# Packed probability blocks, paired value products and single banks in a fused attention and feed-forward kernel

## The chip, the cores and the metric

The kernel runs on one core of a Trainium2 chip. The metric is the device time of one execution in microseconds (us), the median of the runs shown. All data are fp32 in memory; some products take their operands as fp32r, a form that TensorE reads in one pass, where fp32 takes two (two records for each product in the trace).

## The reference

x is (2, 1024, 512), that is 2048 rows of 512. One layer: causal attention with 16 heads of 32, a residual and a layer norm, then a feed-forward part with the signs of its weights, a residual and a layer norm.

```python
qkv = jnp.einsum('bsd,ed->bse', x, w_qkv) + b_qkv          # heads of 32
scores = jnp.einsum('bhqd,bhkd->bhqk', q, k) / math.sqrt(Hd) + causal
out = jnp.einsum('bhqk,bhkd->bhqd', jax.nn.softmax(scores), v)
x = layernorm(x + jnp.einsum('bsd,ed->bse', out, w_out) + b_out)
hidden = relu(jnp.einsum('bsd,hd->bsh', x, sign(up_w)) * up_scale)      # 2048 wide
x = layernorm(x + jnp.einsum('bsh,dh->bsd', hidden, sign(down_w)) * down_scale * output_scale)
```

## The kernel before

**Order.** The kernel first makes a list of tasks. Each has the engines it may run on with estimated costs, a due time (`place`), and the tiles that it reads and writes. `Plan.schedule` (from L104) plays these through, engine by engine, earliest due first, and fixes each engine's order and each tile's buffer. The instructions are then issued in that order (`tc.manual_schedule`); at run time each engine takes its own in order, with semaphore waits. A tile class has so many equal buffers (`slots`), and its tiles get them in the order of their first use. So a change of an estimate moves instructions on all engines.

**Attention** goes in 8 chunks (two batches, four groups of four heads; 128 columns of q, k and v each). For a chunk, `project` makes four L494 products for k and q (each four matmuls of 512 columns, fp32) and 32 value blocks (L531). Keys and queries are split into a high and a low fp32r part (ScalarE L571 and VectorE L576 for keys; VectorE L515, then POOL L554 and L559 for queries). `stack` copies the parts by DMA (L450) into `stacks`, where a head's four parts lie on 128 partitions: 32 DMAs a chunk. The projection of chunk c+1 runs among the attention of chunk c. Chunk 0 is cut in two: rows 0 to 511 have plain fp32 scores (L708) from unsplit k and q, so that attention can begin before stacks exist; 48 stack DMAs of 64 KB for the rest are issued alternately by SP and ScalarE (`BOTH`).

A chunk goes through 8 tiles i of 128 query rows. A tile's heads come in units of 4, 2 or 1, as i grows. For a unit: scores (L727 or L708) into one of two PSUM tiles of two banks (`d0`, `d1`); the mask (L743) and the row maximum (L753) on VectorE; Exp with its row sum on ScalarE (L759); a reciprocal (L770); the scaling of probabilities on POOL (L776); transposes on TensorE (L798) into a bank; a copy to `probsT` by ScalarE or VectorE (L432, L434). After the units of a tile, `values` issues its products as one task: 4(i+1) matmuls of 32 columns (L822), two records each, into one bank, and VectorE adds the bias (L837). `probs` has 4 buffers of 1024 columns and `probsT` 8 buffers of 8 blocks, whatever a unit needs.

**Between.** After a batch's last chunk, `output` multiplies by w_out (L875), adds the residual rows and takes statistics; `normalise` scales (L913).

**Feed-forward** goes in 4 blocks of 512 rows. For each of 16 hidden tiles: eight up-products (L987), ReLU on ScalarE (L998), a split on VectorE (L1004, L1009), and down-products (L1024) into four 512-wide halves of `d0` and `d1`, one for each 128 rows. The last hidden tiles' down-products (4 of them in the last block) come row tile by row tile. Then for each row tile: scale (L1038, VectorE), residual (L1046, on POOL; the very last on VectorE), statistics (L1052, L1057), root (L1062, ScalarE), L1068, scaling (L1073), and a DMA out. These y rows have 3 buffers. Most DMAs are issued by SP.

Of the kernel before, what the change touches and what calls it, by code (L numbers as in the profile page):

```python
# [10 lines left out]
F32 = mybir.dt.float32  # L11
# [15 lines left out]

LAG = 6.0
# [12 lines left out]
GBPS = 220.0  # L41


class Tile:


    def __init__(self, plan, cls, after=()):
        self.cls, self.after = cls, after
        self.users, self.left, self.end = [], 0, 0.0
        self.slot = None  # L50
        self.parts = {}
        self.at = len(plan.classes[cls]["tiles"])
        plan.classes[cls]["tiles"].append(self)
# [12 lines left out]
class Plan:  # L66
# [8 lines left out]
    def tile(self, cls, after=()):  # L75
        return Tile(self, cls, after)
# [33 lines left out]
    def schedule(self):  # L110
# [15 lines left out]
        dma, order = 0.0, []  # L126
        blocked = []
# [5 lines left out]
        def lacks(t, now):  # L133

            at = 0.0
            for x in t.tiles:
                if x.slot is not None:
                    continue
                c = self.classes[x.cls]
                if c["next"] != x.at or not c["free"] or c["held"] >= c["most"] or any(a.left for a in x.after):  # L140
                    return None
                at = max([at, min(c["free"])[0]] + [a.end for a in x.after])
            return at
# [5 lines left out]
        while count < len(self.tasks):  # L149
# [37 lines left out]
            for x in t.tiles:  # L187
                if x.slot is None:
                    c = self.classes[x.cls]
                    pick = min(c["free"])  # L190
                    c["free"].remove(pick)
                    x.slot = pick[1]
                    c["next"] += 1
                    c["held"] += 1
                    opened = True
# [3 lines left out]
            if t.size:  # L199
                dma = max(dma, now + 1.7) + t.size * 1.024 / GBPS  # L200
                t.end = dma
            else:
                t.end = now + until
# [13 lines left out]
            for x in t.tiles:  # L217
                x.left -= 1
                x.end = max(x.end, t.end + 0.15)
                if not x.left:  # L220
                    self.classes[x.cls]["free"].append((x.end, x.slot))
                    self.classes[x.cls]["held"] -= 1
                    opened = True
# [10 lines left out]
def kernel(  # L234
# [86 lines left out]
    def place_for(stack, name, n, kind=F32, side="left"):  # L321
# [9 lines left out]
    doubles = [psum.tile([P, 2 * TB], F32, tag=f"d{k}", name=f"d{k}") for k in range(2)]  # L331
# [14 lines left out]
        "pr": views(a_pr, (2 * TB,)),  # L346
        "pt": views(a_pt, (8, P)),
# [19 lines left out]
        "pd": [d[:, k * TB : (k + 1) * TB] for d in doubles for k in range(2)],  # L367
        "pu": singles,
        "y": views(a_v, (D,))[:3],
        "dsc": views(a_v, (D,))[3:4],  # L370
# [8 lines left out]
    def reopen(cls):  # L379

        if cls == "raw" or cls == "xt" and homes["xt"][0] is None:
            right.close()
            xt = place_for(right, "xt0", 2 * NC * TB, F32R, "right")
            homes["xt"][:1] = views(xt, (2, NC, TB), F32R)
            raw = place_for(right, "raw", NC * TB, side="right")
            homes["raw"] = views(raw, (NC, TB))
        else:
            left.close()
            xt = place_for(left, "xt1", 2 * NC * TB, F32R)
            homes["xt"][1:] = views(xt, (2, NC, TB), F32R)  # L390
            homes["hf"] = views(place_for(left, "hf", 4 * TB), (TB,))
            hid = place_for(left, "hid", 12 * TB, F32R)
            homes["hh"] = views(hid, (TB,), F32R)[:6]
            homes["hr"] = views(hid, (TB,), F32R)[6:]

    def of(t):
        if homes[t.cls][t.slot] is None:
            reopen(t.cls)
        return homes[t.cls][t.slot]

    rows_at = {"x1": views(a_x1, (NQ, D))[0], "xT": views(a_x, (NQ, D))[0]}

# [25 lines left out]
    BOTH = {"SP": (0.6, 0.6), "ACT": (0.5, 0.5)}  # L428
# [12 lines left out]
    all_of = {cls: [] for cls in homes}  # L441

    def new(cls, after=()):
        t = plan.tile(cls, [y for c in after for y in all_of[c]])
        all_of[cls].append(t)
        return t
# [196 lines left out]
    def first_half():  # L643
# [9 lines left out]
        for c in range(NC):  # L653
            dma(
                -100, lambda c=c: of(w)[:, c, 1, :], lambda c=c: w_qkvT[ts(c, P), D : D + P], 64,
                writes=[w[1, c]], queue=act_queue,
            )
# [10 lines left out]
        v, kq = new("v"), new("pt")  # L668
        rows = lambda n: of(kq)[:, 4 * n : 4 * n + 4, :].rearrange("p a b -> p (a b)")
# [6 lines left out]
    def second_half():  # L676

        kq, v = plain[0, 0]
        st, hl = new("st"), new("hl")
        place = pace(-10, 6, 16 * 3)  # L680
        split(hl, 0, lambda: of(kq)[:, 4:8, :].rearrange("p a b -> p (a b)"), [kq[1]], -20)
        stack(st, 1, hl, 0, 0, TB, lambda: -20, BOTH)
        ps = product(0, 0, 1, TB, place)
        split_keys(0, 0, hl, TB, ps, -10)
        stack(st, 1, hl, TB, TB, TB, lambda: -20, BOTH)
        ps = product(0, 0, 0, TB, place)
        qh, full = new("hl"), new("full")
        with_bias(0, 0, 0, lambda: of(full), [full[0]], ps, -10)
        split(qh, 0, lambda: of(full), [full[0]], -10)
        stack(st, 0, qh, TB, 0, TB, lambda: -20, BOTH)  # L690
        values_of(0, 0, v, TB, place)
        made[0, 0] = st, v
# [7 lines left out]
    def scores(b, e, i, heads, at):  # L700
        G, N, W = len(heads), (i + 1) * P, 2 * TB // len(heads)
        sc, nm, pr, sums = new("sc"), new("nm"), new("pr"), new("sums")
        if (b, e) in plain and i < NQ // 2:
            kq = plain[b, e][0]

            def fn(_):
                for j, u in enumerate(heads):
                    nc.tensor.matmul(  # L708
                        of(sc)[:, j * W : j * W + N],
                        lhsT=of(kq)[ts(u, HD), i, :],  # L710
                        rhs=of(kq)[ts(u, HD), 4 : 5 + i, :].rearrange("p a b -> p (a b)"),
                        start=True,
                        stop=True,
                    )
# [41 lines left out]
        for j in range(G):  # L756
# [3 lines left out]
                    of(pr)[:, j * W : j * W + N],  # L760
# [12 lines left out]
        for j in range(G):  # L773
# [3 lines left out]
                    of(pr)[:, j * W : j * W + N],  # L777
                    of(pr)[:, j * W : j * W + N],
# [9 lines left out]
    def transposes(i, heads, pr, at):  # L788
        W = 2 * TB // len(heads)
        blocks = [(j, j * W + k * P) for j in range(len(heads)) for k in range(i + 1)]  # L790
        pt = new("pt")
        for g in range(0, len(blocks), 4):
            some = blocks[g : g + 4]
            tp = new("tp")
            for k, (j, c) in enumerate(some):
# [3 lines left out]
                        of(tp)[:, k, :], of(pr)[:, c : c + P], ident  # L799
# [6 lines left out]
                lambda g_, g=g, m=m, tp=tp: copied(g_, of(pt)[:, g : g + m, :], of(tp)[:, :m, :]),  # L806
# [6 lines left out]
    def values(b, e, i, each, at):  # L813
        if (b, i) not in atT:
            atT[b, i] = new("atT")
        to, v, rows = new("po"), (made.get((b, e)) or plain[b, e])[1], atT[b, i]
        each = each[::-1]

        def fn(_):
            for k in range(i, -1, -1):  # L820
                for u, pt, c in each:
                    nc.tensor.matmul(  # L822
                        of(to)[ts(u, HD), 0, :],
                        lhsT=of(v)[:, k, ts(u, HD)],
                        rhs=of(pt)[:, c + k, :],
                        start=(k == i),
                        stop=(k == 0),
                    )

        plan.task(  # L830
            {"PE": (0.14 + 0.218 * (i + 1), 0.2 + 0.218 * (i + 1))}, fn, at,
            [v[t] for t in range(0, (i + 1) * P, TB)] + [pt[0] for _, pt, _ in each],
            updates=[to[0]], count=8 * (i + 1), label="po",
        )
        plan.task(
            dve(0.345),
            lambda _: nc.vector.tensor_scalar(  # L837
                of(rows)[:, e, :],
                of(to)[:, 0, :],
                bqk[:, 2 * NC + e : 2 * NC + e + 1],  # L840
                None,
                ALU.add,
            ),
            at - FAST, [to[0]], [rows[e]], label="at",
        )

    def attend(b, e, i, base):


# [7 lines left out]
        values(b, e, i, each, base - 2)  # L857
# [110 lines left out]
    def feed_forward(up, dn, dsc, base):  # L968
        UNIT = 2.0

        def block(tb):
# [7 lines left out]
            for f in range(NFC):  # L979
                pu, hf = new("pu"), new("hf", ["pr", "pt"])  # L980
                hh, hr = new("hh", ["pr", "pt"]), new("hr", ["pr", "pt"])
                at = start + f * UNIT
# [50 lines left out]
            for t in range(TPB):  # L1033
                y, st, m, pd, rows = new("y", ["v"]), new("st6"), new("st6"), pds[t], x1[b]
# [8 lines left out]
                adder = dve(0.692) if final and t + 1 == TPB else pool(1.264)  # L1043
                plan.task(
                    adder,
# [26 lines left out]
                    dve(0.546),  # L1072
                    lambda _, m=m, y=y: nc.vector.tensor_scalar(  # L1073
# [15 lines left out]
    for at, (b, e) in enumerate(chunks):  # L1089
# [3 lines left out]
        for i in range(NQ):  # L1093
            attend(b, e, i, base + i * (i + 1) / 2)
        if e == NC - 1:

            x1[b] = new("x1" if b < B - 1 else "xT")
            for i in range(NQ):
                there = base + (i + 1) * (i + 2) / 2 + LAG
                output(b, i, pace(there, there + 4, 16))  # L1100
# [96 lines left out]
```

## Time and profile before

| | us |
|---|---|
| median of 3 runs | 784.16 (783.38 to 786.16) |
| profiled execution, its own time | 780.83 |
| its span | 779.0 |
| attention, up to the first feed-forward product | about 523 |
| feed-forward, to the end | about 256 |

| engine | busy us |
|---|---|
| TensorE (PE) | 758.6 |
| VectorE (DVE) | 519.8 |
| ScalarE (ACT) | 378.9 |
| GpSimd (POOL) | 261.6 |

In the profile a group reads: line, engine, operation, output<-input by the program's names, shape, count. "A <- B: 2.2, 1, 2.2" among the waits means that A's engine sat idle for A until B was done: total us, times, longest. PEld is the loading of weights, which overlaps products. In the chain a piece starts where the piece before it ended, or at what released it; SPq and ACTq are DMA issues.

### The profile page before, as it was taken

The numbers are of one execution on the slowest core, as the hardware profiler recorded it, in microseconds if no ns is written. First come the engines' busy times: TensorE is split into PE (matmuls) and PEld (weight loads), VectorE is DVE, ScalarE is ACT, GpSimd is POOL, SyncE is SP. The second block draws the span as 40 slices with busy tenths as digits, with TensorE's granted clock in tenths as the row PEclk, the third lists the DMA queues.
The fourth block names the chain that finished last, engine by engine and source line by source line (L and its number), as shares of the span: only waits on it lengthen the run. The fifth ranks groups of instructions, "written<-read, shape, count | busy, mean of one in ns | idle before, by whom it ended". The sixth has DMA issues, their size and how long they took to land.

```text
span 779.0 us, 15429 instructions
## 1 busy us (share of the span) xinstructions
PE 758.6 (97%) x5864; PEld 568.4 (73%) x5864; DVE 519.8 (67%) x1083; ACT 378.9 (49%) x841; POOL 261.6 (34%) x329
## 2 busy tenths in 40 slices
PE   8899899999999999999999999999999999999994
PEld 4567768868855775786876876668777887777883
DVE  1678598688777767888878879966336337337325
ACT  1366468667644454566666678654222222222111
POOL 2336346346435443535544545440002002002001
PEclk9999999999999999999999999999999999999998
DMA  8535625226533522634504423332001001001001
GB/s 232 116 82 126 178 61 129 70 60 138 170 77 73 137 58 49 146 89 109 110 2 109 110 64 131 135 120 97 1 0 55 1 0 55 1 0 41 14 0 54
DMA packets 38120, 62.35 MB, mean 80 GB/s; under 512 B 6048, under 2 KB 18336, under 8 KB 38048
## 3 DMA queue, kind: packets, MB, share of 16 engines
q1 hardware_dynamic: 35616, 59.08, 29.5%
q10 hardware_dynamic: 2400, 2.30, 1.2%
q8 instruction: 46, 0.75, 0.4%
q14 instruction: 26, 0.21, 0.1%
q0 software_dynamic: 32, 0.01, 0.0%
HBM read 24.66 MB, written 4.19 MB: 37 GB/s over the span
## 4 chain that ended last, share of the span: by engine, by line
PE 87%; DMA 3%; SPq 3%; DVE 3%; POOL 1%; ACTq 1%; ACT 1%; issue 1%; POOLq 0%; DVEq 0%
PE s L987 15%; PE d L1024 15%; PE s L798 15%; PE s L494 12%; PE d L727 9%; PE s L822 8%; PE s L875 7%; PE s L531 6%; SPq L450 3%; DMA stacks<-wqkv 1%; ACTq L450 1%; PE s L938 1%; DVE small L753 1%; DMA xT<-in_xT 1%; DVE probsT L434 1%
## 5 line engine op out<-in xcount | busy, mean ns | idle before, releaser
L776 POOL TENSOR_SCALAR probs<-probs,small 128x128 f32<-128x128 f32 (+7 forms) x256 | 189.7, 750 | 251.9 <-DVE small L770 216.4
L759 ACT ACTIVATE probs<-d,small 128x128 f32<-128x128 f32 (+7 forms) x256 | 189.2, 749 | 90.0 <-DVE small L770 22.5
L753 DVE TENSOR_REDUCE small<-d 128x1 f32<-128x640 f32 (+9 forms) x178 | 180.0, 1016 | 2.8
L798 PE MATMUL s<-ident,probs 128*128 128x128 f32 x1152 | 164.0, 274 | 0.3 <-POOL probs L776 0.3
L798 PEld LDWEIGHTS s<-ident,probs 128*128 128x128 f32 x1152 | 133.1, 140 | 36.0 <-issue 22.9
L432 ACT COPY probsT<-s 128x512 f32<-128x512 f32 (+3 forms) x195 | 96.0, 520 | 91.1 <-PE s L798 81.6
L1024 PE MATMUL d<-stacks,hid 128*128 128x512 f32 x512 | 134.6, 399 | 0.8 <-DVE v L1038 0.8
L987 PE MATMUL s<-xt,stacks 128*128 128x512 f32 x512 | 134.2, 400 | 0.0
L727 PE MATMUL d<-stacks 128*128 128x512 f32 (+3 forms) x368 | 129.7, 437 | 4.5 <-DMA stacks<-wqkv 2.2
L494 PE MATMUL s<-xT,wqkv 128*128 128x512 f32 x256 | 129.0, 597 | 1.0 <-DMA xT<-in_xT 1.0
L998 ACT ACTIVATE hf<-s,ups 128x512 f32<-128x512 f32 x64 | 44.0, 688 | 167.1 <-PE s L987 167.1
L1024 PEld LDWEIGHTS d<-stacks,hid 128*128 128x128 f32 x512 | 93.8, 188 | 25.5 <-DVE v L1038 2.0
L1004 DVE CAST hid<-hf 128x512 fp32r<-128x512 f32 x64 | 27.4, 428 | 126.6 <-ACT hf L998 126.6
L987 PEld LDWEIGHTS s<-xt,stacks 128*128 128x128 f32 x512 | 94.4, 188 | 23.2 <-issue 1.0
L434 DVE COPY probsT<-s 128x512 f32<-128x512 f32 (+3 forms) x150 | 86.6, 592 | 19.2 <-PE s L798 16.6
L727 PEld LDWEIGHTS d<-stacks 128*128 128x128 f32 x368 | 60.0, 190 | 44.5 <-issue 26.6
L743 DVE TENSOR_TENSOR d<-d,mask 128x128 f32<-128x128 f32 (+2 forms) x178 | 62.3, 354 | 32.3 <-PE d L727 27.1
L822 PEld LDWEIGHTS s<-probsT,v 128*32 128x32 f32 x2304 | 59.0, 109 | 28.5 <-issue 7.9
L822 PE MATMUL s<-probsT,v 128*32 128x128 f32 x2304 | 76.2, 275 | 0.0
L531 PE MATMUL s<-wqkv,xT 128*128 128x128 f32 x512 | 71.3, 275 | 0.0
L531 PEld LDWEIGHTS s<-wqkv,xT 128*128 128x128 f32 x512 | 66.0, 192 | 6.5 <-issue 5.0
L875 PE MATMUL s<-wout,atT 128*128 128x512 f32 x128 | 64.5, 597 | 0.2 <-DVE xt L950 0.2
(63 smaller groups left out, 489.3 us busy)
## 6 DMA issues: line engine op xcount, KB each, us to landing
stacks<-wqkv SPq DMA_DIRECT2D x224, 128.0 KB, 2.4
wqkv<-in_w_qkvT SPq DMA_DIRECT2D x22, 256.0 KB, 3.6
xT<-in_xT SPq DMA_DIRECT2D x16, 256.0 KB, 4.5
rows<-in_x SPq DMA_DIRECT2D x16, 256.0 KB, 2.8
raw<-in_up_wT SPq DMA_DIRECT2D x4, 1024.0 KB, 5.0
out<-v SPq DMA_DIRECT2D x16, 256.0 KB, 2.0
raw<-in_down_wT SPq DMA_DIRECT2D x2, 1024.0 KB, 5.2
atT<-in_down_wT SPq DMA_DIRECT2D x2, 1024.0 KB, 6.5
```

Of the source, the lines that this page charges most:

```text
L432: nc.scalar.copy(dst, src)
L494: nc.tensor.matmul(of(ps).rearrange("p a b -> p (a b)"), lhsT=of(w)[:, c, n, :], rhs=of(xt)[:, c, t0 : t0 + TB], start=(c == 0), stop=(c = ...
L531: nc.tensor.matmul(of(ps)[:, t, :], lhsT=of(xt)[:, c, t0 + t * P : t0 + (t + 1) * P], rhs=of(w)[:, c, 2, :], start=(c == 0), stop=(c == NC ...
L727: nc.tensor.matmul(of(sc)[:, j * W + k0 : j * W + k1], lhsT=of(st)[:, 0, u, ts(i, P)], rhs=of(st)[:, 1, u, k0:k1], start=True, stop=True,)
L753: lambda _: nc.vector.tensor_reduce(of(nm)[:, :G], sc3()[:, :, :N], AX.X, ALU.max, negate=True),
L759: lambda _, j=j: nc.scalar.activation(of(pr)[:, j * W : j * W + N], of(sc)[:, j * W : j * W + N], AF.Exp, bias=of(nm)[:, j : j + 1], accum ...
L776: lambda _, j=j: nc.gpsimd.tensor_scalar(of(pr)[:, j * W : j * W + N], of(pr)[:, j * W : j * W + N], of(sums)[:, j : j + 1], 1.0, ALU.mult ...
L798: lambda _, k=k, c=c, tp=tp: nc.tensor.transpose(of(tp)[:, k, :], of(pr)[:, c : c + P], ident),
L822: nc.tensor.matmul(of(to)[ts(u, HD), 0, :], lhsT=of(v)[:, k, ts(u, HD)], rhs=of(pt)[:, c + k, :], start=(k == i), stop=(k == 0),)
L875: lambda _, c=c: nc.tensor.matmul(bank(py), lhsT=of(a)[:, c, :], rhs=of(wout)[:, c, :], start=(c == 0), stop=(c == NC - 1),),
L987: lambda _, f=f, c=c, n=n, pu=pu: nc.tensor.matmul(of(pu), lhsT=of(up)[:, f // TPB, c, ts(f % TPB, P)], rhs=of(xt)[:, n, c, :], start=(c = ...
L1024: lambda _, f=f, t=t, n=n, h=h: nc.tensor.matmul(of(pds[t]), lhsT=of(h)[:, ts(t, P)], rhs=of(dn)[:, f // 4, f % 4, :], start=(f == 0 and n ...
```

## The change

The diff has six parts.

1. **Rings.** `pr` and `pt` are no longer 4 and 8 equal buffers but rings of 32 and 64 blocks of 128 columns in the same memory. A unit takes only its G(i+1) blocks, contiguous, and blocks come free in order of taking. Exponentials are packed next to each other.
2. **Two tiles in one run.** `attend` holds back the value products of tiles 0, 2 and 4 and issues them with those of the next tile, in one task and one bank; not for tiles 0 to 3 of chunk 0. The last chunk takes its tiles in the order 0, 1, 2, 7, 6, 5, 4, 3.
3. **First stacks.** All of chunk 0's stack DMAs are issued by SP. The first key weights come in two DMAs in place of four.
4. **Single banks.** When the down-products begin, the pool of `d0` and `d1` is closed and four one-bank tiles are opened in its place.
5. **y rows** lie in the old `atT` area, 8 buffers. In the last block the residual of the first three row tiles may go to VectorE or POOL, and their scaling too. The last block's up-products are due 6 us earlier (`HURRY`).
6. **The planner** counts 200 GB/s, 2.3 us to landing and eight DMAs in flight, where it had 220, 1.7 and no limit.

The core of the diff:

```diff
+TOGETHER = (0, 2, 4)
+LAST = [0, 1, 2, 7, 6, 5, 4, 3]
+HURRY = 6.0
...
-GBPS = 220.0
+GBPS = 200.0
+LANDING = 2.3
+LANES = 8
...
+    def room(self, c, x):
+
+        live, n = c["live"], x.blocks
+        if not live:
+            return 0
+        head, tail = live[-1].slot + live[-1].blocks, live[0].slot
+        if head > tail:
+            return head if head + n <= c["ring"] else 0 if n <= tail else None
+        return head if head + n <= tail else None
...
-        "pd": [d[:, k * TB : (k + 1) * TB] for d in doubles for k in range(2)],
+        "pd": [None] * 4,
         "pu": singles,
-        "y": views(a_v, (D,))[:3],
-        "dsc": views(a_v, (D,))[3:4],
+        "y": views(a_at, (D,)),
+        "dsc": views(a_v, (D,))[:1],
...
+        elif cls == "pd":
+            wide.close()
+            narrow = wide.enter_context(tc.tile_pool(name="narrow", bufs=1, space=PSUM))
+            homes["pd"] = [
+                narrow.tile([P, TB], F32, tag=f"pd{k}", name=f"pd{k}") for k in range(4)
+            ]
...
+    rings = {
+        "pr": (a_pr, 4 * 2 * TB // P), "pt": (a_pt, 8 * 2 * TB // P)
+    }
...
-        stack(st, 1, hl, 0, 0, TB, lambda: -20, BOTH)
+        stack(st, 1, hl, 0, 0, TB, lambda: -20)
...
+        pr = new("pr", blocks=G * (i + 1))
...
-                    of(pr)[:, j * W : j * W + N],
+                    of(pr)[:, j * N : (j + 1) * N],
...
-    def values(b, e, i, each, at):
+    def values(b, e, some, at):
...
+            for n, (i, each) in enumerate(some):
+                for k in range(i, -1, -1):
+                    for u, pt, c in each[::-1]:
+                        nc.tensor.matmul(
+                            of(to)[ts(u, HD), n, :],
+                            lhsT=of(v)[:, k, ts(u, HD)],
+                            rhs=of(pt)[:, ts(c + k, P)],
+                            start=(k == i),
+                            stop=(k == 0),
+                        )
...
-        values(b, e, i, each, base - 2)
+        waiting.append((i, each))
+        if not hold_back:
+            values(b, e, waiting[:], base - 2)
+            waiting.clear()
...
-                at = start + f * UNIT
+                at = start + f * UNIT - (HURRY if final else 0)
...
-                adder = dve(0.692) if final and t + 1 == TPB else pool(1.264)
+                both = {**dve(0.692), **pool(1.264)}
+                if not final:
+                    both = pool(1.264)
                 plan.task(
-                    adder,
+                    both if t + 1 < TPB else dve(0.692),
...
+        tiles = list(range(NQ))
+        if at + 1 == len(chunks):
+            tiles = LAST
+        begin, past = {}, base
+        for i in tiles:
+            begin[i] = past
+            attend(b, e, i, past, i in TOGETHER and not (at == 0 and i < NQ // 2))
+            past += i + 1
```

## The prediction

> **What bounds the kernel now.** I read the page first: busy time by engine, then the chain that ended last.
>
> ```profile
> PE 758.6 (97%) x5864; PEld 568.4 (73%) x5864; DVE 519.8 (67%) x1083; ACT 378.9 (49%) x841; POOL 261.6 (34%) x329
> PE 87%; DMA 3%; SPq 3%; DVE 3%; POOL 1%; ACTq 1%; ACT 1%; issue 1%; POOLq 0%; DVEq 0%
> ```
>
> TensorE is busy for 97% of the span and makes 87% of the chain. The next engine is VectorE with 67%. A gain can come from three places alone: cheaper instructions in TensorE's stream, TensorE waits that go, and the ends, where TensorE has nothing to do. The table by stretch says how much lies at the ends (columns: stretch, its length, busy time with counts, granted clock, DMA share, GB/s).
>
> ```profile
> 1.00:42.00 41.00, 37.51 (x202) 22.65 (x203) 16.15 (x38) 11.14 (x36) 10.60 (x21) 1.00 0.70 183
> 523.00:763.00 240.00, 240.00 (x1056) 191.34 (x1055) 108.69 (x210) 59.02 (x92) 18.13 (x13) 1.00 0.07 23
> 763.00:779.00 16.00, 5.11 (x21) 3.41 (x19) 10.53 (x23) 1.65 (x5) 3.74 (x3) 0.80 0.17 66
> ```
>
> The feed-forward stretch is solid: 1024 products at 232 to 233 ns from end to end are 238.3 of its 240 us. Nothing is to be had there before its last 10 us. The first 42 us leave 3.5 us idle, the last 16 leave 10.9.
>
> But "busy" hides one thing. Records of a pipelined engine overlap, so a slow passage between two kinds of matmul counts as busy. The timeline of TensorE alone shows it (start, length, group):
>
> ```profile
> 78.45 0.60 PE L798 MATMUL s<-ident,probs 128*128 128x128 f32 x4
> 78.98 1.74 PE L822 MATMUL s<-probsT,v 128*32 128x128 f32 x56
> 80.65 0.66 PE L798 MATMUL s<-ident,probs 128*128 128x128 f32 x4
> 81.14 1.06 PE L531 MATMUL s<-wqkv,xT 128*128 128x128 f32 x8
> ```
>
> Subtract ends. The run of value products (L822, 32-column tiles) ends 1.67 us after the transposes before it, and the four transposes after it take 0.59 us more, where four transposes in a stream take 4 x 0.109 = 0.44. By record: the first L822 record of a run ends 227 ns after the record before it (64 runs, 226 to 228), within a run the mean is 25.5 ns, so entering costs 0.20 us. Leaving costs 0.15 us to a transpose (259 against 109 ns, 21 times) and 0.20 to a 512-wide score product (428 against 232, 27 times), 0.18 on the mean. A run costs 0.38 us beside its work; 64 runs, 24 us.
>
> The waits of TensorE that the trace does show, the six longest:
>
> ```profile
> PE d L727 <- DMA stacks<-wqkv: 2.2, 1, 2.2
> PE d L708 <- ACT probs L759: 2.0, 1, 2.0
> PE s L648 <- POOL ident masks.py:199: 1.5, 1, 1.5
> PE d L727 <- DVE small L770: 1.3, 1, 1.3
> PE s L494 <- DMA xT<-in_xT: 1.0, 1, 1.0
> PE d L1024 <- DVE v L1038: 0.8, 1, 0.8
> ```
>
> And the end of the chain, in order of time (start, length, what):
>
> ```profile
> 762.70 2.83 PE d L1024 x12
> 765.55 0.76 DVE v L1038
> 766.39 2.53 POOL v L1046 x2
> ...
> 770.43 2.04 DMA out<-v
> ...
> 772.57 0.76 DVE v L1038
> ```
>
> The last tile's y (L1038) starts at 772.57, not when its product ends (768.96), because it waits for an output DMA to give back one of three y buffers.
>
> **Value products of two tiles in one run.** The same 1152 products are issued, in 42 runs instead of 64 (counted in the changed kernel's instruction order): 21 pairs in chunks 1 to 7 and one in chunk 0. Summing the passages with this trace's own record distances over both orders, 22 entries fewer save 22 x 0.20 = 4.4 us and the exits that go save 3.6. Sum: **8.1 us**, all on the path, as TensorE bounds these stretches. The cost: a pair's first tile is held until the second's transposes are done, so its rows and probsT blocks live longer. I cost that at nothing: after the last transpose of a pair the stream holds 0.8 us at least and 1.55 in the middle before the run (1.0 and 1.55 before), above a copy's 0.59 to 0.69. If that cover is gone in each run, 22 x 0.3 = 6.6 us come back.
>
> **Rings of blocks (probabilities and their transposes).** Exponentials are packed, so a tile holds G*(i+1) blocks and not always eight; no instruction is added. The trace of before shows no TensorE wait that names a full buffer. Bound: 0 to 1 us gain; in-order release could cost as much. I take 0. Other transitions in the changed stream differ by under 1.4 us in sum; 0 as well.
>
> **First stacks from one queue.** ScalarE no longer issues 27 stack DMAs. Its own rows say what they cost: exponentials waited 20.3 us in three pieces (L759 <- stacks), and TensorE waited 2.0 us at 28.7 for one of them (L708 <- L759). That 2.0 goes. The price is on SP, which now issues 32 key stacks, then chunk 1's three weight loads, then 16 query stacks. Seven of these stacks took 4.40 us there, 0.63 each. Here a rule of the Trainium skill speaks on the other side: page "DMA: Bandwidth & Descriptors", section "Issuing engines are not separate DMA queues", says that issuing from several engines saves only the sequencer's time, usually small beside the transfer. By it one queue would cost nothing and the stacks would land as early as before. By the row, the first 16 took 11.9 to 17.9 on two queues and take 16 x 0.63 = 10 us on one, to 22; the second 16 to 32; weights to 34. The query split now stands behind 16 normalisations on POOL, so its first part is ready at about 36.6; 16 more issues reach 46.7, and 2.1 us to landing give 47.0 for the first head and 48.8 for the last. I take the row. Cover: the first score product on stacks has moved back in the stream, from 39.6 to 47.0 us of work, some 49 us with the start's waits. So 0 to 2 us of new wait; I take 1.0. Chunk 1's projection, which needs the weights landed at about 36 to 37.6, starts near 39: covered, and 2 to 3 us if that slips.
>
> The start also loads the key weights in two DMAs, not four, and interleaves the key and query products of the first half. The 1.0 us wait for xT is bound by the transfer (0.84 busy in the first 20 us); I leave it.
>
> **Later stacks.** The 2.2 us wait at 84 goes: between the last query product of chunk 1 and its first score product the stream holds 23.5 us, where it held 15.4. For chunks 2 and 3 it is 27 instead of 12, so the wait of 1.3 there goes as well, with a hidden 0.4. For chunks 5 to 7 it falls from 19 to 22 down to 14.4 to 15.0. What is needed: bias 0.74, split 0.61 + 1.26, 16 issues x 0.62, landing 2.4, 15.0 if nothing overlaps; 12.0 to 13.5 sufficed in chunks 2 and 3. New wait 0 to 3 us for the three; I take 1.0. Together: 2.0 + 2.2 + 1.7 - 1.0 - 1.0 = **3.9 us**.
>
> **Single banks for down-products.** In the last block the y of row tile 0 waited for row tile 1 (one two-bank buffer), and TensorE waited 0.8 us for a reader of the other bank (1.1 by record ends). That goes: **1.0 us**. In the other blocks the matching stalls lie on weight loads and hide.
>
> **Eight output rows and the end.** The tail after the last product is 779.0 − 769.0 = 10.1 us. Without the buffer wait, VectorE does after the last product: y 0.75, three left-overs of earlier tiles (0.16 + 0.68 + 0.18), add 0.69, stats 0.69, aggregate 0.18, wait for the root 0.36, two reciprocals 0.32, two scalings 1.1, with gaps about 5.2. From ln's end to the span's end were 779.0 − 776.1 = 2.9. Tail 8.2 us, **1.9 us** less. Moving the last block's up-products forward puts 44 down-products in one stretch, so tiles 0 to 2 finish early; that is what keeps left-overs this small. If POOL's share is late, at most 1.9 is lost.
>
> **The reordered last chunk** (tiles 0, 1, 2, 7 to 3) changes which work trails. Hidden waits of 0.1 to 0.5 us between 489 and 514 sum to 1.3; gain or loss within that, taken as 0.
>
> **Sum.** 8.1 + 3.9 + 1.0 + 1.9 = 14.9. A denser stream leaves the other engines less time (transposes follow their scores by 6.7 us at least for tile 1, before 8.5; VectorE's 0.82 busy share from 392 to 523 rises with it), so I give back 0.5. The profiled execution goes from 779.0 to 764.6 span, its time from 780.83 to about 766.4. The three timed runs have a median of 784.16, 3.3 above it; the same 14.4 off gives **769.8 us**.
>
> **The rivals.**
>
> A, only the runs pay: waits taken away return elsewhere, as each buffer or stack is late in turn. For it: TensorE's waits are short and have six different causes. Against: four causes are removed by name. 784.2 − 8.1 − 1.9 = 774, chance 0.22.
>
> B, more than I count: every hidden wait in attention (some 4 us beyond those listed) goes as well: 765, chance 0.13.
>
> C, slower, one mechanism: SP's single queue before the first stacked score. 48 issues at r us each put the last landing at 11.9 + 48r + 1.9 + 2.1. At 0.63 that is 46, inside 49. SP's 32 stacks of 128 KB took 29.3 us with their waits, 0.92 each: at that rate 60 us, so 11 us of idle TensorE, and from 0.98 on the wait eats all 14.4. SP's other 14 stacks of the start took 18.5 us, 1.32 each, as they waited for ScalarE's share; halfway, at 1.1, the landing is at 69, the wait 20 us and the time 784.2 - 14.4 + 20 = 790. Against: the slow ones waited for data or for the other queue, the undisturbed seven took 0.63. Chance 0.07.
>
> D, nothing measurable (gains and new waits cancel): 784, chance 0.05.
>
> **How the numbers follow.** Main case 0.53, 769.8, own range 766 to 773. The range 763 to 779.5 takes in A and B and leaves out C, D and the edges, some 0.17. A change of 0.3% (2.4 us) is about what can be told from none: faster 0.88, within 0.05, slower 0.07.
>
> **What would show it.** Value-product runs still entered at 227 ns, 42 of them; ScalarE's issues of stacks gone; TensorE's waits without L708 <- L759 and without a reader of the other bank; the first stacked score near 49 us; last product near 756.5 and a tail near 8 us. I am wrong if TensorE idles over 3 us before the first stacked score, if score products of chunks 5 to 7 wait over 1 us each for stacks, or if runs begin late because their copies are.

## The result and the profile after

The changed kernel takes 771.98 us, the median of 4 runs (771.77 to 774.42), where the kernel before takes 784.01 beside it (783.38 to 786.16). The ratio is 0.9849, 95% interval 0.9822 to 0.9876: faster by 1.5%. From one profiled execution to the other the span fell by less, from 779.0 to 770.2 us. The page of the changed kernel, busy time by engine and the chain that ended last:

```profile
PE 752.4 (98%) x5864; PEld 571.3 (74%) x5864; DVE 519.6 (67%) x1087; ACT 379.4 (49%) x841; POOL 257.1 (33%) x325
PE 51%; DVE 5%; SPq 1%; ACT 1%; issue 1%; DMA 1%; POOL 0%; POOLq 0%; DVEq 0%; ACTq 0%
```

TensorE is still the bound. (The chain could be followed back over only part of the span, so 51% is no fall.) Its longest waits, and a run of value products of two tiles (L888, before L822) in the timeline:

```profile
PE s L859 <- POOL probs L838: 1.9, 2, 1.5
PE s L703 <- POOL ident masks.py:199: 1.5, 1, 1.5
PE d L789 <- DMA stacks<-wqkv: 1.4, 1, 1.4
PE d L789 <- ACT probs L821: 1.4, 2, 0.9
PE s L549 <- DMA wqkv<-in_w_qkvT: 1.0, 1, 1.0
PE s L859 <- DVE probsT L489: 0.9, 1, 0.9
PE d L770 <- DVE probsT L570: 0.9, 1, 0.9
PE pd L1099 <- DVE hid L1079: 0.5, 2, 0.3
```

```profile
71.27 0.65 PE L789 MATMUL d<-stacks 128*128 128x512 f32 x2
71.85 2.61 PE L888 MATMUL s<-probsT,v 128*32 128x128 f32 x88
74.39 0.73 PE L789 MATMUL d<-stacks 128*128 128x512 f32 x2
```

The old waits are gone: no score product waits for an exponential that stack DMAs held up (L708, 2.0 us), none for chunk 1's stacks (2.2), no down-product for a reader of the other bank (0.8). New ones stand in their place. The 88 records of tiles 4 and 5 (the second line) end 2.54 us after the product before them, one entry and one exit for the two.

The end, in the chain (start, length, what):

```profile
756.86 5.61 PE pd L1099 x24
762.51 0.74 DVE atT L1113
...
766.30 0.55 DVE atT L1150
```

The last y (L1113) starts as its product ends, with no wait for an output DMA; the tail is 770.2 - 762.5 = 7.7 us.

I use one more measure below. "Waits by record ends" are the distances between the ends of neighbouring TensorE records beyond what is usual for that pair of kinds in the first trace, summed. They include short waits that overlapped records hide, and a slow clock; runs of value products and of row-tiled scores (chunk 0's plain ones, on 32 rows of the array) are left out. Before: 11.3 us. After: 10.8. So of the profiled pair's 8.8 us only 0.5 came from waits: 2.4 are in the tail, and the rest, 5.9, in TensorE's own stream.

### The profile page after: what moved, and what is told of

Its sections match the earlier page's. It is cut to its first block, busy times and chain, and to the rows that moved or that the text cites. A ratio compares the mean times of both kernels' runs of the same rounds, so it can differ in the third digit from the quotient of the medians.

```text
span 770.2 us, 15411 instructions
## 1 busy us (share of the span) xinstructions
PE 752.4 (98%) x5864; PEld 571.3 (74%) x5864; DVE 519.6 (67%) x1087; ACT 379.4 (49%) x841; POOL 257.1 (33%) x325
## 4 chain that ended last, share of the span: by engine, by line
PE 51%; DVE 5%; SPq 1%; ACT 1%; issue 1%; DMA 1%; POOL 0%; POOLq 0%; DVEq 0%; ACTq 0%
PE s L1062 14%; PE pd L1099 14%; PE s L859 6%; PE s L888 4%; PE d L789 4%; PE s L549 3%; PE s L950 3%; PE s L586 2%; SPq L505 1%; DVE small L1129 1%; PE s L1013 1%; DVE x L988 1%; DVE atT L1113 1%; DMA stacks<-wqkv 1%; DVE atT L1150 0%
## 5 line engine op out<-in xcount | busy, mean ns | idle before, releaser
L815 DVE TENSOR_REDUCE small<-d 128x1 f32<-128x768 f32 (+9 forms) x178 | 180.2, 1016 | 3.0
L1099 PE MATMUL pd<-stacks,hid 128*128 128x512 f32 x512 | 133.4, 399 | 0.5 <-DVE hid L1079 0.5
L789 PE MATMUL d<-stacks 128*128 128x512 f32 (+2 forms) x368 | 123.7, 426 | 2.8 <-DMA stacks<-wqkv 1.4
L1099 PEld LDWEIGHTS pd<-stacks,hid 128*128 128x128 f32 x512 | 94.3, 188 | 24.1 <-DVE hid L1079 1.4
L888 PEld LDWEIGHTS s<-probsT,v 128*32 128x32 f32 x2304 | 60.4, 110 | 18.7 <-issue 5.4
L586 PE MATMUL s<-wqkv,xT 128*128 128x128 f32 x512 | 72.9, 276 | 0.0
L888 PE MATMUL s<-probsT,v 128*32 128x128 f32 x2304 | 71.6, 274 | 0.2 <-DVE probsT L489 0.2
```

Source lines behind the costliest of these rows:

```text
L586: nc.tensor.matmul(of(ps)[:, t, :], lhsT=of(xt)[:, c, t0 + t * P : t0 + (t + 1) * P], rhs=of(w)[:, c, 2, :], start=(c == 0), stop=(c == NC ...
L789: nc.tensor.matmul(of(sc)[:, j * W + k0 : j * W + k1], lhsT=of(st)[:, 0, u, ts(i, P)], rhs=of(st)[:, 1, u, k0:k1], start=True, stop=True,)
L815: lambda _: nc.vector.tensor_reduce(of(nm)[:, :G], sc3()[:, :, :N], AX.X, ALU.max, negate=True),
L888: nc.tensor.matmul(of(to)[ts(u, HD), n, :], lhsT=of(v)[:, k, ts(u, HD)], rhs=of(pt)[:, ts(c + k, P)], start=(k == i), stop=(k == 0),)
L1099: lambda _, f=f, t=t, n=n, h=h: nc.tensor.matmul(of(pds[t]), lhsT=of(h)[:, ts(t, P)], rhs=of(dn)[:, f // 4, f % 4, :], start=(f == 0 and n ...
```

## The experiments

Each was timed beside the kernel before, whose median was 782.1, 783.1, 781.8 and 783.5 us in the four groups of runs. So a ratio is given with each time: where ratio and median say different things, both stand.

**The kernel before, again** (no edit).

> The kernel before, unchanged, profiled once more. The first profiled execution of it took 780.83 us while four timed ones had a median of 784.01; the change gained 8.8 us from profile to profile and 12.0 from median to median. Theory 1 (executions of the kernel before scatter, and its first profile was a quick one): another profile with a span near 782, the same tail of 10.1 us after the last product, and TensorE waits some 3 us above the 11.3 us counted in the first profile. Rival (the timed runs carry something outside the span): span again near 779 and timed median 784.

Measured: 782.49 us beside 782.12, ratio 0.9992 (0.9973 to 1.0011), 14 executions from 779.12 to 784.73. The profiled span was 781.6, granted clock 0.991 where the first profile had 0.996. The stretches of the new profile say where:

```profile
20.00:30.00 10.00, 8.05 (x50) 5.48 (x51) 4.35 (x10) 2.25 (x9) 1.21 (x4) 0.99 0.58 131
30.00:37.00 7.00, 7.00 (x34) 4.35 (x32) 2.56 (x5) 3.28 (x11) 3.40 (x6) 0.52 0.04 9
```

and the same stretches of its first profile:

```profile
20.00:30.00 10.00, 8.03 (x49) 5.16 (x47) 4.27 (x9) 2.01 (x9) 1.46 (x4) 1.00 0.61 138
30.00:37.00 7.00, 7.00 (x62) 4.20 (x61) 5.17 (x12) 3.49 (x11) 4.82 (x8) 1.00 0.20 47
```

The column after the five engines is the granted clock: TensorE ran at half clock for some 7 us. The two executions have the same order, so their records can be matched one by one: the second is 0.3 us ahead at 29.9 us, 2.8 behind at 34.6, and 2.6 behind at the last product. That stretch is the 2.6 us between the spans. The timed executions of the kernel before scatter with the clock in the same way: the eight granted 0.989 took 785.8 us on the mean, the five granted 0.994 took 780.4. The changed kernel's had 0.996 to 0.998.

The slow stretch follows the one in which TensorE waited 2.0 us for ScalarE; the kernel with pairs alone, which has the same start and the same wait (1.9), shows it too (0.994). So theory 1 was right that the first profile was a quick one and wrong on where: the tail (10.1) was equal and the waits elsewhere nearly. That this start's idle time makes the clock fall is likely and not proved: the first profile had the same wait and kept its clock. The Trainium skill's page "TensorE: Matmul & The Clock Gate", Part 1, gives half rate after a window of some 3.4 us idle; here no wait was longer than 2.0.

**Pairs broken by one transpose**, order unchanged.

```diff
             for n, (i, each) in enumerate(some):
+                if n:
+                    nc.tensor.transpose(of(to)[:, 3, :], ident, ident)
                 for k in range(i, -1, -1):
```

> The changed kernel in exactly its own order, but in each of the 22 paired runs one dummy transpose (identity into an unused quarter of the same bank) stands between the two tiles. Theory 1 (a passage between the 128-column and the 32-column form costs TensorE time that nothing hides): each break costs 259 + 227 - 89 ns, by the record distances of the profile after, so 22 x 0.397 = 8.7 us more: 780.7. Rival (matmul ends are modelled, so the distances are no real time): only the transpose's own 0.109 us, 2.4 us in all: 774.4.

Measured: 779.26, ratio 0.9961 (0.9944 to 0.9977); span 776.8, 6.6 us above the changed kernel's. The profile shows 64 runs, entered at 226 to 229 ns as before but for two that waited. The 8.7 us were laid in, and waits by record ends fell from 10.8 to 8.7, so 2.1 were absorbed. The rival's 2.4 is out: passages are real time on the path.

**No pairs**: `TOGETHER = ()`.

> The changed kernel without holding back (each tile its own run: 64 runs), all else as changed, planned anew. Theory 1 (the runs carry 6.7 us: 22 entries x 0.138 and the exits 3.6): 778.7, with 2 to 3 us either way because the planner lays other work differently. Rival (the prediction's 8.1): 780.1. Second rival (the named waits carry the gain, the runs little): 774.

Measured: 776.03, ratio 0.992 (0.9895 to 0.9945), span 774.3, 4.1 above the changed one's. Waits by record ends 8.4 against 10.8, tail 8.0 against 7.7: the stream without waits and tail grew by 6.2 us. The runs carry nearly what theory 1 says, and more than a third of it is paid back in waits.

**Pairs alone on the kernel before** (the new `values`, `waiting` and `hold_back`; fixed buffers).

> The kernel before with paired value products alone (42 runs), its fixed buffers, queues, tail and estimates as before. Theory 1 (runs worth 6.7 us, waits refall but their sum stays near 11 us): 777.3. Rival (holding back with fixed buffers makes new waits that eat the gain, so the rings are needed): 782 or more, with TensorE waits of 5 us above before's.

Measured: 776.38, ratio 0.992 (0.9894 to 0.9947): about 6 us, theory 1. Waits by record ends 12.1 with a half-clock stretch in it. Pairs don't need rings.

**First stacks from two queues again**: `stack(..., lambda: -20, BOTH)` in three places.

> The changed kernel with the first stacks issued by SP and ScalarE in turn again, as before the change, all else as changed, planned anew. Theory 1 (ScalarE's issues hold up exponentials, TensorE idles some 2 us near 28 us and, where its idle time falls so, its clock is halved for some microseconds): ScalarE shows waits of 10 us or more for stack DMAs before 45 us, the time is 2 us up where the clock holds and 4 to 5 where it doesn't, and executions scatter by 3 us or more: 774 to 777. Rival (one queue is no gain, ScalarE's share only moves): 772 within 1, and no wider scatter than the changed kernel's.

Measured: 772.18, ratio 0.9863 (0.9827 to 0.9898): 0.2 us more than the changed kernel by the medians, 1.1 by the ratios. The executions ran from 769.51 to 775.84, so the scatter came as theory 1 said, but its median didn't. ScalarE's waits before 60 us:

```profile
ACT probs L821 <- DMA stacks<-wqkv: 12.1, 2, 6.8
...
ACT wqkv L626 <- DMA stacks<-wqkv: 7.0, 1, 7.0
```

They are back nearly in full (19.1 us, before 20.3) and cost the whole nothing that is clear of the scatter: TensorE was busy for all of 20 to 30 us, where in before it idled 2.0. In this profile the row-tiled scores wait 1.4 and 0.5 us near 39 and 48 us instead, and a 1.6 us wait for stacks at 389 is 1.0.

**The old end**: two-bank halves, three y buffers, old engines, no `HURRY`.

> The changed kernel with the down-products in halves of the two-bank buffers again, three y buffers, last additions and scalings on the old engines and up-products of the last block not moved forward. Theory 1 (these parts carry the tail of 7.7 against 10.1 us and the 1.1 us wait between the last down-products): 3.4 us more, 775.4. Rival (the tail is bound by VectorE's chain and the output DMA alone): under 1 us more.

Measured: 773.4, ratio 0.9878 (0.9852 to 0.9904); 1.4 us more by the medians, 2.3 by the ratios, not 3.4. The pieces came as expected: tail 10.2 us, and the wait between the last down-products back (1.1). But the last product ended 1.7 us earlier than in the changed kernel. Two waits of 0.5 us by record ends, at 587 and 649 (down-product for VectorE's `hid`), are absent here and stand in all new-end kernels: there the new end gives part of its gain back. The 1.6 us at 389 is absent too, and that is not the end's doing: every engine's order is the same in both kernels up to 577 us. The last two stacks landed 3.9 and 3.6 us after their issue in the changed kernel's profile, the last one 2.4 after in this one. So the end is worth 2.4 + 1.1 - 2 x 0.5 = 2.5 us in the profiles. Banks, rows and earlier up-products were not separated.

**Four tiles in one run**: `TOGETHER = (0, 1, 2, 4)`.

> The changed kernel with tiles 0 to 3 in one run of value products (and 4 with 5; in the last chunk 0, 1, 2 and 7): 35 runs for 42. Theory 1 (each run that goes saves 0.14 at the entry and 0.15 to 0.2 at the exit): 7 x 0.3 = 2.1 us less, 769.9, if waits keep their sum of 11 us; planner's other order may take or give 2. Rival (the longer holding back fills the rings and makes transposes wait): 774 or more, with waits for probabilities' copies above before's.

Measured: 773.88, ratio 0.988 (0.9853 to 0.9907). Runs 35, and the last product ends no earlier (762.9): waits by record ends rose to 13.0, in many pieces between 461 and 504 (transposes). The rival's time, within 0.1; that full rings are the reason is not shown.

**The planner's estimates alone** on the kernel before.

```diff
-GBPS = 220.0
+GBPS = 200.0
+LANDING = 2.3
+LANES = 8
...
+                start = max(now, lanes[0])
+                free[e] = start + busy
+                dma = max(dma, start + LANDING) + t.size * 1.024 / GBPS
...
```

> The kernel before with the planner's three new DMA estimates alone (200 GB/s, 2.3 us, eight in flight); no operation is changed, only orders. Theory 1 (waits are where estimate and chip part, a new plan moves them and keeps their sum): 782 within 2. Rival (the better estimates remove the waits for stacks of 2.4 and 1.5 us): 778, with no wait of a score product for stacks.

Measured: 777.23, ratio 0.9929 (0.99 to 0.9957). Not one operation was changed, and 5.9 us went. TensorE's longest waits in its profile:

```profile
PE s L654 <- POOL ident masks.py:199: 1.5, 1, 1.5
PE d L1030 <- DVE v L1044: 0.8, 1, 0.8
PE d L714 <- ACT probs L765: 0.8, 1, 0.8
PE d L733 <- ACT probs L765: 0.7, 1, 0.7
PE s L804 <- POOL probs L782: 0.6, 1, 0.6
```

No score product waits for stacks, and waits by record ends are 5.8 us against 11.3. The rival. Part of the 5.9 goes with the clock: this kernel was granted 0.992 to 0.996, before beside it 0.990 in the middle. Against before's five executions at 0.994 (780.4) 3.2 us are left, and from first profile (0.996) to this one (0.995) the span fell by 4.8.

**No rings**: `blocks=8` for every tile of both rings.

> The changed kernel with every tile of probabilities and of transposes taking eight blocks of its ring, which is the fixed buffers of before (4 and 8); packing and all else as changed. Theory 1 (TensorE's waits of 10.8 us in the changed kernel against 5.8 with the planner's estimates alone come from where the new plan puts units beside the normalisation and VectorE's copies, not from rings): 772 within 2, waits near 11 us. Rival (rings let TensorE run further ahead and are needed for pairs): 775 or more, waits 14 us or more. Second rival (rings are what brought the new waits): 768.

Measured: 768.8, ratio 0.9825 (0.9798 to 0.9852), 767.82 to 768.93: below every execution of the changed kernel, by 3.2 us between the medians, 1.9 by the ratios. Waits by record ends 7.6. The second rival's time. The changed kernel waits 1.8 us at 190 for POOL and 3.2 us from 308 to 317; here 0.4 and 1.1 remain at those places.

**Plain order of the last chunk**: `LAST = list(range(8))`.

> The changed kernel with the last chunk's tiles in the order 0 to 7. Theory 1 (that order is worth within 1.5 us either way: the hidden waits between 489 and 514 were 1.3 us before and are 1.6 after): 772 within 1.5, with all waits before 440 us unmoved as the plan up to there is the same. Rival (the order lets the last tiles' short chain hide, so undoing it costs): 774 or more.

Measured: 772.11, ratio 0.9864 (0.9839 to 0.9889). Theory 1, but for one wait: the order is the changed kernel's up to 455 us, and yet the wait of 1.6 us at 389 (by record ends) is 1.0 here. Its length belongs to the execution, not to the plan.

**The parts that paid, together** (fixed buffers, plain order, two queues and four key-weight DMAs; estimates, pairs and the new end).

> Only the parts that earlier runs showed to pay, in one kernel: the planner's estimates, paired runs, single banks, eight y rows and the new end; fixed buffers, the last chunk's plain order, first stacks from two queues and four key-weight DMAs as before. Theory 1 (each part keeps its worth and the estimates' waits of 5.8 us stay): 777.2 - 6.7 - 3.4 = 767. Rival (waits belong to the whole plan, a new plan draws them anew): 770 to 774, waits 9 to 12 us.

Measured: 768.57, ratio 0.9826 (0.9802 to 0.985). Below the changed kernel, 1.6 above the sum; waits by record ends 9.3, not 5.8. Parts' gains in waits do not add.

**Another plan with rings**: `LANDING = 2.5`.

> The changed kernel, rings and all, with one planner estimate moved (2.5 us to landing for 2.3), so that the same tasks are laid in another order and no operation is changed. It asks whether the 3.2 us that fixed buffers gained were the rings' or the draw of another plan. Theory 1 (the draw: any new plan places the waits anew): the time moves by 1 to 4 us, the waits at 190 (1.8 us) and at 308 to 317 (3.2 us) go or change. Rival (rings let units run so that they collide at those places): 772 within 0.7, both waits still there.

Measured: 771.36, ratio 0.9851 (0.9837 to 0.9864). The wait at 190 went, the one at 308 to 317 stayed, and the tail came out at 8.8. Neither theory alone.

## Why the prediction was right, and which terms were off

The forecast was 769.8 us in a range of 763 to 779.5; 771.98 came. The direction holds, and so does the mechanism of the runs and of the end; that of the waits does not. Its sum was 14.4 us. Between the profiles 8.8 came, and the last product ended at 762.5, not near 756.5. Between the medians it was 12.0, because most timed executions of before, by the clocks on record, also carry a half-clock stretch, and the changed kernel's do not. The forecast counted those 3.3 us above the first profile as if they would stay. That they went made up for more than half of what the sum lacked: the median came nearer than the reasoning, by luck. Term by term:

| term | predicted | measured |
|---|---|---|
| value-product runs | 8.1 | 6.7 by record distances, 6.2 without pairs |
| named waits at the start and for stacks, net | 3.9 | removed as named, given back elsewhere |
| wait between the last down-products | 1.0 | 1.1 gone, two of 0.5 new in earlier blocks |
| tail | 1.9 | 2.4 (10.1 to 7.7) |
| rings | 0 | the plans with them 2 to 3 slower, cause open |
| the planner's estimates | not costed | by themselves 5.9 by medians, 4.8 by profiles |

- **Runs: right mechanism, mis-sized.** I subtracted the mean record distance in a run, 25.5 ns, from the entry's 227. But the distances come in fours, about 7, 7, 7 and 89 ns, and a second tile starts at an 89. So a joined entry saves 227 - 89 = 138 ns, 3.0 us for 22, and the exits 3.6, some 6.7 in all. The order-preserving experiment confirms the price, and no-pairs finds 6.2.
- **First stacks: the trade was as drawn, its value wasn't there.** SP's 32 key stacks took 21.2 us, 0.66 each (0.63 predicted); the first stacked score came at 49.8 (some 49) and waited for no stack, where I had allowed 1.0. The row was right here against the "usually small" of the Trainium skill's page "DMA: Bandwidth & Descriptors", section "Issuing engines are not separate DMA queues". But in place of the exponential's 2.0 us, the first scores now wait 0.9 for the query bias (L770 <- L570), which I had not listed, and putting two queues back cost nothing clear. What the old start did cost beside the 2.0 us, half clock in some executions, the first profile of before did not show. Nor is it the single queue that keeps the clock: the kernel of the parts that paid uses two and was granted 0.997 to 0.999.
- **Later stacks: right but for a sign.** The waits of chunks 1 to 3 went; one of 1.4 us came, at 389, in chunk 6, one of the three I had as tight (1.0 taken for all). Over 1 us was one of my signs of being wrong; other executions of the same order up to there waited 0.7 us or not at all.
- **The wrong step: new waits taken as 0.5 us beyond the listed ones.** With that the waits were to fall by 3.9 + 1.0 - 0.5 = 4.4 us; by record ends they fell by 0.5, from 11.3 to 10.8, so 3.9 came back. The largest stand where the schedule is densest: at 190 TensorE waits for a scaling on POOL, whose reciprocal stood behind two copies and a maximum on VectorE; from 308 to 317 the normalisation of batch 0 meets chunk 5. VectorE's timeline there, of the changed kernel, and POOL's:

```profile
308.38 1.58 DVE L988 TENSOR_SCALAR x<-x,small 128x512 f32<-128x512 f32 x2
309.88 0.73 DVE L570 TENSOR_SCALAR wqkv<-s,bqk 128x512 f32<-128x512 f32 x1
310.54 0.15 DVE L832 RECIPROCAL small<-small 128x1 f32<-128x1 f32 x1
310.61 0.27 DVE L489 COPY probsT<-s 128x128 f32<-128x128 f32 x1
310.79 3.65 DVE L988 TENSOR_SCALAR x<-x,small 128x512 f32<-128x512 f32 x4
314.37 0.41 DVE L489 COPY probsT<-s 128x256 f32<-128x256 f32 x1
```

```profile
310.85 1.17 POOL L838 TENSOR_SCALAR probs<-probs,small 128x768 f32<-128x768 f32 x1 [1.17 <-DVE small L832]
311.96 0.79 POOL L609 CAST wqkv<-wqkv 128x512 fp32r<-128x512 f32 x1
312.84 1.32 POOL L614 TENSOR_TENSOR wqkv<-wqkv 128x512 fp32r<-128x512 f32 x1
```

Four scalings, planned at 0.543 us each, took 3.65. Singly they started at 310.79, 311.25, 312.21 and 312.96; the first took 0.53 us, and each of the other three started while one of these POOL instructions ran and ended 0.28 us after it. A copy of transposes stood behind them and TensorE behind the copy (0.9). My rival A, waits that return elsewhere, is what the profile shows; its 774 missed by 2 us, as the fall of the medians also holds the clock.

- **Rings: no gain, and perhaps a loss.** I took 0 from "0 to 1 us gain". The two kernels with fixed buffers beside pairs and estimates took 768.6 and 768.8, the six with rings 771.4 to 773.9. But each is one plan, and two of the six share the changed kernel's order up to 577 and 455 us. Whether rings as such let units collide or these plans happened to is open: another plan with rings removed one of the two waits and kept the other, and the kernel of the parts that paid, with fixed buffers, has 2.2 us of waits from 307 to 317.
- **The estimates: left out.** I read the DMA constants as the means of the other parts, and by themselves they were the second largest part. The waits that they took away were in my list, credited to other parts.

## What to carry to other kernels

Where one engine is busy 97% of the time, price the passages between its instruction kinds from the ends of neighbouring records, and take the distance that the saved instruction will really have, not a mean over a pattern. A wait that is removed from a static order is worth its length only when the rest of the order stays: estimates in the planner were worth 3 to 6 us here, as much as a redesigned stage, and waits of separate improvements didn't add. Profile the kernel before twice and compare the granted clock: one execution may miss what its timed runs contain.

## What the runs showed of the hardware that was not expected

- In some executions TensorE's clock was halved for 7 us (0.52 granted from 30 to 37 us) after a stretch in which it was busy for 8.05 of 10 us.
- VectorE's scaling of 512 columns in SBUF took 0.53 to 0.55 us with POOL idle or when it started before POOL's instruction. When POOL's instruction was already running, the scaling ended 0.28 us after it, however long that took: up to 1.49 us. This fits all 8 scalings of batch 0 in the changed kernel (L988, mean 0.83) and all 8 in the kernel before (L913, mean 0.65).
- The same scaling with subtract and multiply on POOL took 2.07 us, where the planner counts 0.69. It lies off the path. VectorE's last addition beside it took 0.90 us in place of 0.69, but another addition beside the first of these two kept 0.69.
